# A list-scheduled transformer block: routed experts in freed places, one factor to ScalarE, and a new set of due times

## The chip, the cores and the metric
The kernel runs on one core of one Trainium2 chip, in one launch. The metric is the device time of that core in microseconds. Its engines are called by the short names that the profile uses: PE is TensorE (PEld its weight loads), DVE is VectorE, ACT is ScalarE, POOL is GpSimd, SP is SyncE, whose queue issues all the kernel's DMAs.

## The reference
64 sequences of 256 tokens with 256 features, each with a context of 120 tokens, pass through four steps, each added to the tokens under a tanh gate:

```python
x = x + tanh(g_xattn[0]) * L0_xattn(layernorm(x), ctx)   # 16 heads of 64, softmax over 120
x = x + tanh(g_ffn[0])   * L0_ffn(layernorm(x))          # 8 experts, gate softmax, threshold 0.1
x = x + tanh(g_xattn[1]) * L1_xattn(layernorm(x), ctx)   # 16 heads of 16
x = x + tanh(g_ffn[1])   * L1_ffn(layernorm(x))          # 8 routed experts, two of them per token
```

The last step has 512 routing rows only, so it applies to the first 512 tokens (one group). For them each routed expert computes, with LIMIT = 7 and alpha = 1.702:

```python
gate = minimum(x @ Wg + bg, LIMIT)
up   = clip(x @ Wu + bu, -LIMIT, LIMIT)
y    = ((up + 1) * gate * sigmoid(alpha * gate)) @ Wd + bd      # weighted and summed by token
```

All arithmetic is in float32.

## The kernel before
**Work and order.** Tokens are taken in 32 groups of two sequences (512 tokens, four tiles of 128). One group is one *turn*, and its work falls into three stages: *front* (keys and values of the context, first attention), *middle* (`ffn0`, the gated experts) and *back* (second attention, then the store). The group with the routed experts, group 0, is taken as the third from last. Its own fourth step, `ffn1`, comes at the very end as the stage *routed*.

**The planner.** The code does not issue instructions directly. Each piece (four matmuls, one copy, one DMA) is a `step` with an engine, a cost in us, the steps it comes after, the buffers it opens and uses, and a due time. The class `Plan` runs a list schedule over all steps: whenever an engine falls idle in the model, the ready step with the earliest due time is taken, if its buffers are free. The instructions are then emitted in that order, and each engine executes its own in that order. The due time of a step comes from its place in its stage: `begin + length * (PE time before it / PE time of the stage)`, in turns, less a correction from the table `EARLY` (thousandths of a turn, one number per step; positive is earlier). The constants `FRONT`, `MIDDLE`, `BACK` and `ROUTED` hold begin and length.

**Tile shapes on PE.** Most matmuls use the full 128x128 array; scores, values and gate logits use smaller tiles, and each has a `mode` (`scores0`, `values0`, `scores1`, `values1`, `logits`). The planner adds a cost when the mode changes, and shifts due times: `ALONE` when the only ready tiled step would enter from full work, `PAIR` when there are several, `BACK` for going back to full, `OTHER` from one tiled mode to another.

**Softmax weights** are transposed by DMA (`by_dma`): POOL splits the words into halves (tile `hv`), SP issues the transpose into `tu`, ACT joins the halves into `aT` or `aTb` (line 733). Layer norms of the middle and back, and of later fronts, go the same way. In the model a transpose occupies SP for 2.6 us and is seen 2.0 us after that.

**Buffers** are rings of places. Those that matter here: `x_ring` (4 token places), `xn_ring` (2, normalized tokens, 1024 words a row), `exf_ring` (4, first attention's weights `ex`), `q0_ring` (3, queries `qT`), `v0_ring` (2), `ao0_ring` and `k0_ring` (1 each), `late_ring` (2, of which second attention uses three in turn), `sp_ring` (2 score places in PSUM) and `mm_ring` (4 PSUM banks).

**Routed experts** (`ffn1`). An expert's gate and up matrix is loaded into a place of `v0_ring`, the down matrices into the one place each of `ao0_ring` and `k0_ring`. For each half `m` of the hidden features: a PE step for gate and one for up; DVE takes each out of PSUM with bias and upper limit into a place of `exf_ring` (line 1502); ACT makes a tanh of the gate (line 1511); POOL clips the up factor from below and adds one (line 1518); DVE makes gate times (tanh + 1) (line 1525); POOL multiplies the two factors into a place of `q0_ring` (line 1534). Two PE steps then multiply by the down matrix, and DVE adds to the tokens with the routing weight (line 1564). The loads, and the normalization of the routed tokens, come after `front_done`: the last group's whole front.

Of the kernel before, what the change touches and what calls it, by code (L numbers as in the profile page):

```python
# [13 lines left out]
AF = mybir.ActivationFunctionType  # L14
# [3 lines left out]
P = 128  # L18
D = 256
NQ = 256  # L20
# [16 lines left out]
FRONT, MIDDLE, BACK = (0.0, 1.183), (1.177, 0.93), (1.839, 1.446)  # L37
ROUTED = 6.144
# [3 lines left out]
        -598, -378, -110, -125, -80, 105, 286, 614, 655, -721, 157, 99, -416, -870, -204, 264,  # L42
        -122, 142, -893, -81, -1097, -217, -1070, 136, -768, 416, 276, 99, 625, 512, 251, 565,
        324, 395, -10, 52, -142, -190, -26, 408, 780, 198, -182, 86, -27, -432, 40, 893, 828,
        -519, -46, 248, -49, -395, -279, -29, 632, 812, 1061, 763, -242, 337, 265, -203, 742, 961,
        932, -681, 722, 367, 194, 309, 264, -40, -361, -149, -83, -766, -372, -340, -367, -208,
        -289, -483, -398, -30, 787, 935, -284, -594, 415, -438, -47, 851, 536, -306, -60, 312,
        -214, 279, -581, -1304, -287, -457, -295, -126, -1285, -557, -508, 107, -303, 230, -727,
        -735, -366, -421, -491, 481, 112, -803, 25, 34, -278, -347, 458, 177, -689, -626, -456,
        -883, -321, -547, -840, -697, -1162, -735, -571, -1139, -1160, -491, -1203, -322, -536,  # L50
        -595, -737, -459, -140, -820, -745, -152, 266, 200, -291,
    ],
    "front": [
        243, 272, -206, -364, -216, 241, 53, 106, -149, 513, -137, 189, -424, 1037, -307, -271,
        -85, 67, -427, 13, -118, -471, 50, -39, 390, 203, -231, -469, -807, -273, 207, -264, 703,
        217, 296, 299, 13, 600, 256, -650, -10, -437, -167, 243, 332, 341, 216, 159, -72, 335, 96,
        370, 351, 196, 75, 1040, 364, -197, -303, 280, -478, 232, 35, 77, 105, -225, -473, -384,
        -152, 890, 304, 612, -1015, 634, 408, 258, 342, -115, 671, 252, 76, -125, 66, 60, -307,
        -279, -374, -614, -294, -449, -310, -72, -378, -440, -641, -499, -356, 274, 536, 197,
        -287, 744, 158, 473, 163, -827, 931, 730, -3, -215, -1626, 51, -98, 2, 31, 175, -1228,  # L60
        -672, -648, -422, -406, 392, 731, -68, -169, -1092, -201, -623, -32, -494, 633, -924,
        1305, 84, -517, 373, -1350, 217, -384, -656, 516, -497, 680, 350, 324, 1955, 421, 1294,
        531, 1216, 698, -1274,
    ],
    "middle": [
        -121, -494, 280, 1233, 936, 1977, 1723, 2493, 1181, 484, 955, 763, 1384, 1719, 1131, 1958,
        870, 1018, 1132, 2801, 1132, 1078, 1100, 2346, 1538, 1394, 1665, 1992, 1197, 1040, 964,
        982, 1137, 1192, 1414, 1123, 931, 511, 488, 503, 497, -121, -252, -98, -272, 5, -372,
        -223, -706, -428, -304, -633, -870, -314, -620, -1258, -431, -892, -219, -256, -519, -865,
        -264, -264, -814, -255, -704, -658, -174, -600, -476, -279, -350, -317, -97, 33, -159,  # L70
        -247, -773, -86, -224, -761, 358,
    ],
    "back": [
        776, 1052, 901, 505, 1125, 1001, 1083, 1445, 691, 154, 600, -72, -298, -196, -382, -714,
        -669, -132, 174, -270, -92, -405, 578, 595, 405, 235, 1862, 498, 1543, 217, -311, 62,
        -512, -609, -676, -361, -324, 850, -318, -655, -147, 203, 244, -8, 370, -48, -247, 349,
        -213, -369, -506, 1037, 35, -139, -1632, -791, -1054, -121, -311, 585, -495, -874, 111,
        324, 870, 589, 1263, 263, 142, 863, 667, 170, -501, 902, 17, 406, 1429, 101, -48, -1162,
        -1300, -801, -94, -268, -195, -1010, -726, -590, 210, 990, -81, 290, -303, 506, 68, 155,
        898, 644, 699, 20, -45, -908, -320, -1047, 136, 717, 822, 818, 1051, 1457, 1006, 1157,  # L80
        392, 1644, 605, 1267, 1187, 676, 1428, 749, 611, 384, 193, 2225, -188,
    ],
    "routed": [
        711, 592, 528, 855, -6, -59, -332, -372, 8, -431, -662, -133, 3, -622, -262, -45, -735,
        201, -188, -813, -90, -232, 452, -778, -354, -329, -159, -737, -207, 489, 159, -203, -375,
        -172, 254, -1016, -1038, 703, 698, 1382, 631, 643, 244, 39, 694, 355, -425, 405, -1062,
        656, 3, 123, -237, -528, -600, -368, -817, 554, -108, -226, -58, -181, -634, -1383, -1354,
        -455, -1053, -1286, 800, 184, 1457, 155, 1203, 357, 473, 191, -503, 23, 1480, -93, 2097,
        491, 435, 875, -62, 102, -294, -939, 36, -1066, -1043, 841, -363, 1840, -500, 1298, -771,
        -436, -149, -425, -401, 2073, -917, 2078, 20, -189, -259, -325, -648, -1304, -2133, -761,  # L90
        -1974, -1761, 336, -1255, 1315, -1191, 1517, 51, 714, 863, -214, 39, 1984, -305, 1422,
        -641, -209, 1216, 459, 439, -453, -440, 474, -1091, -893, 1257, -862, 1798, -953, 1308,
        -570, -380, 137, -43, -885, 1373, -840, 1205, -1003, -423, -139, -542, -1195, -2086,
        -2446, -1272, -2493, -2435, 164, -1449, -45, -1537, 330, -301, -906, -62, -1961, -1313,
        -484, -2129, 18, -1342, -1790, -860, -1268, -1911, -2954, -2491, -1495, -2770, -2495, 47,
        -1622, 595, -2026, 212, -186, -243, 352, -546, -1385, 530, -901, 428, 101, -121, 464, 464,
        -164, -892, -1105, -550, -1699, -1435, 883, -848, 1063, -1202, -128, 470, -950, -187,
        -870, -1407, -121, -1037, -40, -803, -982, -63, -1031, -747, -982, -659, 228, -1432, -930,
        1609,
# [7 lines left out]
BY_DMA_SEEN = 2.0  # L107
TURN = "FBM"
HALVES, TURNED, XNS = 2, 2, 2
BEHIND1 = 0  # L110
# [35 lines left out]
class Plan:  # L146
# [10 lines left out]
        "logits": 0.154, "bias": 0.16,  # L157
    }


    ALONE, PAIR, BACK, OTHER = 0.283, -0.055, 0.357, -0.066
# [6 lines left out]
    def step(self, engine, us, emit, after=(), opens=(), uses=(), mode="full", port=False,  # L168
        kind=None, seen=None):
        s = Step(engine, us, emit, after, opens, uses, mode, port)  # L170
        s.due, s.kind, s.seen = self.at, kind, seen or self.SEEN[engine]
        if engine == "PE":
            self.at += us
        self.stage.append(s)
        return s
# [11 lines left out]
    def ordered(self):  # L187
# [7 lines left out]
        port_from = 0.0  # L195
        done = []
# [8 lines left out]
        while events:  # L205
# [15 lines left out]
            while started:  # L221
                started = False
                for e, steps in waiting.items():
# [42 lines left out]
                    heapq.heappush(events, (now + us + s.seen, next(number), s))  # L266
# [18 lines left out]
def kernel(  # L285
# [42 lines left out]
    def ring(name, n, *shape):  # L328
# [19 lines left out]
        ring(name, *((2, P, 8 * P) if which in BY_DMA else (4, P, 2 * NQ)))  # L348
        for name, which in (("aT", "0"), ("aTb", "1"))
# [366 lines left out]
    def by_dma(ex, n, aT, after, which, of_halves=()):  # L716
# [15 lines left out]
        def joined():  # L732
# [9 lines left out]
            "SP", 2.6, lambda: nc.sync.dma_start_transpose(tu.tile, hv.tile),  # L742
            [s], opens=[tu] if of_halves else [tu, aT], uses=[hv, *of_halves], kind="D" + which,
            seen=BY_DMA_SEEN,
# [35 lines left out]
    def add_bias(tk, gated_bias, after):  # L780
        tk.change(
            range(NT), "POOL", 2.385,
            lambda: nc.gpsimd.tensor_tensor(
                tk.x.tile, tk.x.tile,
                gated_bias.unsqueeze(1).to_broadcast([P, NT, D]), ALU.add,
            ),
            after,
        )

    def context0(tk):  # L790
# [31 lines left out]
        for b in range(NB):  # L822
# [29 lines left out]
            vs.append((v, v_in))  # L852
        return kT, kT_in, vs

    def attention0(tk, xnT, xnT_in, kT, kT_in, vs, behind=1):
        nch = NC0 // 2

        def queries(b, hf):
            qTs = []
            for c2 in range(nch // 2):  # L860
# [17 lines left out]
                )  # L878
                s = step(
# [38 lines left out]
        def attend(b, hf, exs, ao):  # L918
            v, v_in = vs[b]
            made = []  # L920
            for u, (ex, s) in enumerate(exs):
# [38 lines left out]
                )  # L960
                c = hf * nch + u * 2
# [71 lines left out]
    def bias_folded():  # L1033
# [39 lines left out]
        s = step("PE", 0.42, gate_mean, gw_in, opens=[ps], mode="logits")  # L1073
# [9 lines left out]
    def ffn0(tk):  # L1083
# [4 lines left out]
        def logits_T():  # L1088
# [13 lines left out]
            mode="logits",  # L1102
# [295 lines left out]
    def ffn1(tk, after):  # L1398
# [42 lines left out]
        ]  # L1441
        xnT = Held(xnT_rings[0])
        xnT_in = layernorm_T(tk, xnT, after, which="routed")
# [3 lines left out]
        for e in range(NE):  # L1447

            def dn_of(e):
# [8 lines left out]
                    after, opens=[] if e % 4 else [dns[e // 4]],  # L1458
# [3 lines left out]
        for e in range(NE):  # L1462
            gu = Held(v0_ring)

            def gu_of(gu=gu):
# [7 lines left out]
                after, opens=[gu],  # L1473
            )
            hTs = [Held(q0_ring) for _ in range(2)]
            hT_in = []
            for m in range(2):
                made = []
                gate, up, sig = Held(exf_ring), Held(exf_ring), Held(aTf_ring)
                for s in range(2):  # L1480
                    ps = Held(mm_ring)

                    def project(m=m, s=s, ps=ps, gu_of=gu_of):
# [11 lines left out]
                    into = up if s else gate  # L1495
                    p = step(
                        "PE", 1.716, project, [*xnT_in, gu_in],
                        opens=[ps, into] if s else [ps, into, sig, hTs[m]], uses=[gu, xnT],
                    )

                    def bounded(e=e, m=m, s=s, ps=ps, into=into):
                        return nc.vector.tensor_scalar(
                            into.tile[:, :TOK], ps.tile, gub_s[:, e, s, m : m + 1], LIMIT,
                            ALU.add, ALU.min,
                        )
# [172 lines left out]
```

## Time and profile before
| what | us |
|---|---|
| median of three runs (lowest, highest) | 3569.85 (3568.73, 3570.05) |
| the profiled execution | 3568.64 |
| its span, first to last instruction | 3566.9 |
| PE busy | 3501.9 |
| DVE, ACT, POOL busy | 2828.2, 2481.6, 2398.9 |
| routed gate and up out of PSUM by DVE (line 1502), 32 instructions | 23.8 |
| PE waits for the routed product on POOL (line 1534), 6 times | 15.0 |

The page's span is the time between the first and the last instruction; the profiled execution's own time has 1.7 us more around it. A line number stands for the place in the code, and since a helper issues nearly all matmuls, they all have line 545: groups are told apart by tiles, as in `mm<-ew,xnT_m` (the gated experts), `mm<-xnT_f,v` (routed gate and up), `mm<-kT,qT` and `mm<-ao,qT` (routed down), `sp<-kbd,late` and `mm<-aTb,vsp` (scores and values of the second attention), `mm<-xnT_m,gw` (gate logits). PE counts as busy over the modelled ends of its matmuls.

### The profile page before, as it was taken

How to read it: one execution, taken by the hardware profiler on the slowest of the kernel's cores; microseconds unless marked ns; L12 is line 12 of the kernel's file. 1: busy time of each engine (PE TensorE's matmuls, PEld its weight loads, DVE VectorE, ACT ScalarE, POOL GpSimd, SP SyncE). 2: the span in 40 equal slices, each digit the busy share in tenths (PEclk: the TensorE clock that was granted, in tenths of full speed). 3: DMA queues.
4: the chain of work that ended last, by engine and by line, in shares of the span. 5: the costliest groups of instructions: out<-in, count | busy, mean ns of one | idle time of the engine just before them, and what ended most of it. 6: DMA issues, size and time to landing. Idle time of an engine off the chain costs nothing.

```text
span 3566.9 us, 52784 instructions
## 1 busy us (share of the span) xinstructions
PE 3501.9 (98%) x20053; PEld 2261.0 (63%) x20053; DVE 2828.2 (79%) x4981; ACT 2481.6 (70%) x2230; POOL 2398.9 (67%) x1625
## 2 busy tenths in 40 slices
PE   7999999999999999999999999999999999999987
PEld 5756666666666666666666666666666666666544
DVE  6677778888777888777888777888877888877776
ACT  4666677777677777677777677777767777767643
POOL 5556667676667776667666667767666777666666
PEclk9999999999999999999999999999999999999998
DMA  6445565555555565555655555555555556555633
GB/s 173 79 83 103 104 113 103 104 110 110 105 109 104 107 115 104 104 108 106 110 109 108 105 102 114 103 106 110 109 100 114 104 107 113 106 102 99 125 71 83
DMA packets 1300861, 378.26 MB, mean 106 GB/s; under 512 B 1266144, under 2 KB 1280896, under 8 KB 1300608
## 3 DMA queue, kind: packets, MB, share of 16 engines
q1 hardware_dynamic: 1300608, 374.90, 54.9%
q8 instruction: 157, 2.57, 0.3%
q14 instruction: 96, 0.79, 0.1%
HBM read 39.80 MB, written 16.78 MB: 16 GB/s over the span
## 4 chain that ended last, share of the span: by engine, by line
PE 84%; DVE 6%; DMA 3%; issue 3%; POOL 3%; ACT 2%; POOLq 0%; SPq 0%; DVEq 0%; ACTq 0%
PE mm L545 74%; PE sp L545 10%; DMA tu<-hv 3%; DVE sum L684 2%; DVE sum L669 1%; POOL hv L724 1%; DVE exb L674 1%; ACT aTb L733 1%; POOL exb L693 1%; ACT aT L733 1%; DVE xt L1187 0%; ACT exb L679 0%; DVE xt L776 0%; DVE ln L571 0%; POOL ex L1518 0%
## 5 line engine op out<-in xcount | busy, mean ns | idle before, releaser
L545 PE MATMUL mm<-ew,xnT_m 128*128 128x512 f32 x2048 | 952.7, 596 | 6.1 <-DVE xt L776 4.1
L733 ACT COPY aTb<-tu 120x2048 uint16<-120x2048 uint16 x256 | 637.5, 2502 | 186.0 <-DMA tu<-hv 184.8
L693 POOL TENSOR_TENSOR exb<-exb,sum 128x960 f32<-128x960 f32 x256 | 460.4, 1803 | 425.4 <-DVE sum L688 420.2
L1187 DVE SCALAR_TENSOR_TENSOR xt<-mm,w_s,xt 128x256 f32<-128x256 f32 x1024 | 486.7, 478 | 265.1 <-PE mm L545 247.1
L733 ACT COPY aT<-tu 120x2048 uint16<-120x2048 uint16 x256 | 636.7, 2505 | 78.7 <-DMA tu<-hv 78.6
L669 DVE TENSOR_REDUCE sum<-sp 128x8 f32<-128x960 f32 x512 | 575.8, 1141 | 113.3 <-PE sp L545 111.1
L693 POOL TENSOR_TENSOR ex<-ex,sum 128x960 f32<-128x960 f32 x256 | 458.2, 1796 | 263.2 <-DVE w_s L1141 132.7
L545 PEld LDWEIGHTS mm<-ew,xnT_m 128*128 128x128 f32 x2048 | 382.2, 190 | 358.1 <-issue 311.5
L545 PE MATMUL mm<-xnT_f,wq 128*128 128x256 f32 x2048 | 489.8, 387 | 0.4 <-DVE xt L1187 0.4
L545 PE MATMUL mm<-wo,ao 128*128 128x256 f32 x2048 | 466.7, 384 | 0.0
L724 POOL COPY hv<-ex 128x1920 uint16<-128x1920 uint16 x256 | 455.2, 1786 | 17.0 <-DMA tu<-hv 12.9
L724 POOL COPY hv<-exb 128x1920 uint16<-128x1920 uint16 x256 | 455.2, 1785 | 6.6 <-DMA tu<-hv 0.3
L545 PEld LDWEIGHTS mm<-xnT_f,wq 128*128 128x128 f32 x2048 | 376.1, 190 | 98.9 <-issue 44.8
L545 PEld LDWEIGHTS mm<-wo,ao 128*128 128x128 f32 x2048 | 381.7, 190 | 79.6 <-issue 31.1
L684 DVE TENSOR_REDUCE sum<-exb 128x8 f32<-128x960 f32 x256 | 287.9, 1136 | 67.8 <-ACT exb L679 67.5
L684 DVE TENSOR_REDUCE sum<-ex 128x8 f32<-128x960 f32 x256 | 289.3, 1141 | 16.4 <-ACT ex L679 16.4
L545 PE MATMUL mm<-wv,ct 128*120 128x512 f32 (+1 forms) x768 | 300.5, 528 | 0.0
L545 PEld LDWEIGHTS sp<-kT,qT 64*128 64x128 f32 x4096 | 242.3, 188 | 87.8 <-issue 74.9
L674 DVE TENSOR_TENSOR ex<-sp,sum 128x960 f32<-128x960 f32 x256 | 289.6, 1143 | 0.6
L545 PE MATMUL mm<-ct,wk 128*128 128x240 f32 x1280 | 289.8, 371 | 0.0
L545 PEld LDWEIGHTS mm<-ct,wk 128*128 128x128 f32 x1280 | 242.0, 191 | 70.5 <-issue 53.3
L674 DVE TENSOR_TENSOR exb<-sp,sum 128x960 f32<-128x960 f32 x256 | 286.1, 1147 | 0.0
(117 smaller groups left out, 4603.3 us busy)
## 6 DMA issues: line engine op xcount, KB each, us to landing
xt<-in_x SPq DMA_DIRECT2D x32, 512.0 KB, 4.3
out_x<-xt SPq DMA_DIRECT2D x32, 512.0 KB, 2.8
tu<-hv SPq DMA_TRANSPOSE x607, 4.4
ct<-in_ctxT SPq DMA_DIRECT2D x32, 240.0 KB, 2.7
v<-in_gu_w SPq DMA_DIRECT2D x8, 512.0 KB, 4.3
ew<-in_expert_w SPq DMA_DIRECT2D x2, 1024.0 KB, 9.6
wk<-in_wkT SPq DMA_DIRECT2D x1, 1024.0 KB
wv<-in_wvT SPq DMA_DIRECT2D x1, 1024.0 KB
```

The costliest lines, as they stand in the source:

```text
L545: return [nc.tensor.matmul(**t) for t in terms]
L669: lambda: nc.vector.tensor_reduce(per_head(0), scores(), AX.X, ALU.max),
L674: lambda: nc.vector.tensor_tensor(weights(), scores(), wide(0), ALU.subtract),
L684: lambda: nc.vector.tensor_reduce(per_head(8), weights(), AX.X, ALU.add),
L693: lambda: nc.gpsimd.tensor_tensor(weights(), weights(), wide(8), ALU.mult),
L724: return copy[APART[which][0]](hv.tile.rearrange("p (h c n) -> p h c n", h=2, c=8)[:, :, :, :n], ex.tile.bitcast(U16).rearrange("p (c n h) ...
L733: return copy[JOINED[which][0]](flat().bitcast(U16).rearrange("p (c n h) -> p h c n", h=2, c=8)[:n], tu.tile[:n].rearrange("p (h c) n -> p ...
L1187: return nc.vector.scalar_tensor_tensor(xs, ps.tile[:, i * D : (i + 1) * D], w.tile[:, t, e : e + 1], xs, ALU.mult, ALU.add,)
```

## The change
- **Routed experts' places.** The products of odd experts go to a token place (`x_ring`), those of even experts stay in `q0_ring`. The factors of the second half (`m = 1`) share one place of `xn_ring`, those of the first stay in two places of `exf_ring`. Places are opened later: the tanh's at the tanh, the product's at the product.
- **When they may begin.** The routed normalization comes after the last group's last query step, the gate and up loads after its last value step, the down loads after its last first-output step, in place of `front_done`.
- **Upper factor.** ACT takes it out of PSUM with its bias, to which DVE adds one once; POOL then clips to (1 - LIMIT, 1 + LIMIT). DVE keeps the gate.
- **Gate tiles.** The mode `logits` is gone; the gate steps have mode `values1`.
- **The model.** Transposes take 1.9 us of SP and are seen 2.4 us later, and none lands within 3.5 us of the one before. The four shifts for tiled steps change.
- **Due times.** New begins, lengths and corrections for all stages; the last group's middle and back have tables of their own.

The numbers of steps and of matmuls per group stay as they are. The core of the diff, without the tables:

```diff
-FRONT, MIDDLE, BACK = (0.0, 1.183), (1.177, 0.93), (1.839, 1.446)
-ROUTED = 6.144
+FRONT, MIDDLE, BACK = (0.0, 1.174), (1.208, 0.757), (1.866, 0.888)
+ROUTED = 6.482
...
-BY_DMA_SEEN = 2.0
+BY_DMA_SEEN = 2.4
...
-        "logits": 0.154, "bias": 0.16,
+        "bias": 0.16,
     }
-    ALONE, PAIR, BACK, OTHER = 0.283, -0.055, 0.357, -0.066
+    SPACED = 3.5
+    ALONE, PAIR, BACK, OTHER = 0.656, 0.033, 0.572, 0.052
...
+                    end = now + us + s.seen
+                    if s.spaced:
+                        end = landed = max(end, landed + self.SPACED)
...
-            "SP", 2.6, lambda: nc.sync.dma_start_transpose(tu.tile, hv.tile),
+            "SP", 1.9, lambda: nc.sync.dma_start_transpose(tu.tile, hv.tile),
...
-            mode="logits",
+            mode="values1",
...
+        up_in = [step("DVE", 0.2, lambda: nc.vector.tensor_scalar(
+            gub_s[:, :, 1, :], gub_s[:, :, 1, :], 1.0, None, ALU.add), gub_in)]
-        xnT_in = layernorm_T(tk, xnT, after, which="routed")
+        xnT_in = layernorm_T(tk, xnT, [front["queries"]], which="routed")
...
-                    after, opens=[] if e % 4 else [dns[e // 4]],
+                    [front["output"]], opens=[] if e % 4 else [dns[e // 4]],
...
-                after, opens=[gu],
-            )
-            hTs = [Held(q0_ring) for _ in range(2)]
+                [front["values"]], opens=[gu],
+            )
+            if e % 2:
+                hTs = [Held(x_ring)] * 2
+            else:
+                hTs = [Held(q0_ring) for _ in range(2)]
...
-                gate, up, sig = Held(exf_ring), Held(exf_ring), Held(aTf_ring)
+                sig = Held(aTf_ring)
+                held = [Held(xn_ring)] * 2 if m else [Held(exf_ring) for _ in range(2)]
...
+                    def biased(ps=ps, factor=factor, b=b):
+                        return nc.scalar.activation(factor(1), ps.tile, AF.Identity, bias=b)
...
+                    if s:
+                        made.append(step("ACT", 0.69, biased, [p, *up_in], uses=uses))
+                    else:
+                        made.append(step("DVE", 0.747, bounded, [p, *gub_in], uses=uses))
...
-                        up.tile[:, :TOK], up.tile[:, :TOK], -LIMIT, 1.0, ALU.max, ALU.add
+                        factor(1), factor(1), 1.0 - LIMIT, 1.0 + LIMIT, ALU.max, ALU.min
...
-        plan.end_stage(turn + MIDDLE[0], MIDDLE[1], EARLY["middle"])
+        plan.end_stage(turn + MIDDLE[0], MIDDLE[1], EARLY[last + "middle"])
...
-        plan.end_stage(turn + BACK[0], BACK[1], EARLY["back"])
+        plan.end_stage(turn + BACK[0], BACK[1], EARLY[last + "back"])
```

`front["values"]`, `front["queries"]` and `front["output"]` are set in `context0` and `attention0` and hold the last such step that was made, that is, the last group's.

## Prediction
> **What bounds the kernel now.** I read the page first, then stretches of 20 us, then TensorE in order of time in one middle turn and in the last 200 us, and last the waits.
>
> ```profile
> span 3566.9 us, 52784 instructions
> PE 3501.9 (98%) x20053; PEld 2261.0 (63%) x20053; DVE 2828.2 (79%) x4981; ACT 2481.6 (70%) x2230; POOL 2398.9 (67%) x1625
> PE   7999999999999999999999999999999999999987
> PEclk9999999999999999999999999999999999999998
> ```
> TensorE is the bound; only the first slice and the last two are not full. There are two places to gain: what TensorE spends inside the full stretches, and the ends.
>
> TensorE inside one middle turn (start us, us, what):
> ```profile
> 1042.85 1.07 PE L545 MATMUL mm<-aTb,vsp 120*32 120x256 f32 x16
> 1043.85 1.99 PE L545 MATMUL mm<-xnT_f,wq 128*128 128x256 f32 x8
> 1045.68 1.89 PE L545 MATMUL mm<-wv,ct 128*120 128x256 f32 x8
> 1047.50 0.64 PE L545 MATMUL mm<-xnT_m,gw 128*32 128x128 f32 x16
> 1048.07 1.98 PE L545 MATMUL mm<-ew,xnT_m 128*128 128x512 f32 x4
> ...
> 1061.61 1.88 PE L545 MATMUL mm<-ew,xnT_m 128*128 128x512 f32 x4
> 1063.42 1.09 PE L545 MATMUL sp<-kbd,late 32*128 32x240 f32 x16
> 1064.44 3.72 PE L545 MATMUL mm<-xnT_f,wq 128*128 128x256 f32 x16
> ```
> Starts tell more than durations. Twelve undisturbed expert products elsewhere (1075.48 to 1080.72, 5.24) give 1.72 for four, against 1.81 before the tiled work at 1063.42: entering costs about 0.09. The eight products from 1043.85 take 1.82; eight clean ones of their size 1.72 (32 output products, 3346.81 to 3353.91, take 7.10 with both sides): leaving costs about 0.1. A second value step behind a first adds 0.86 where one alone adds 1.02: a change of tile shape costs about 0.155. A turn of this plan has 12 entries and 19 groups of one shape, so 12 x 0.2 + 19 x 0.155 = 5.3 us of its 105.6 (gate products start at 1047.50 and, a turn later, at 1153.1). Of 30 such distances 17 are 105.6; others reach 107.0.
>
> The end (20 us rows: busy PE, PEld, DVE, ACT, POOL, clock, DMA), then its TensorE rows, then its waits:
> ```profile
> 3340.00:3360.00 20.00, 20.00 (x103) 12.13 (x102) 15.37 (x32) 12.97 (x9) 12.08 (x9) 1.00 0.62 114
> 3360.00:3380.00 20.00, 12.35 (x60) 6.85 (x59) 9.82 (x28) 10.93 (x8) 10.72 (x11) 0.74 0.87 212
> 3520.00:3540.00 20.00, 13.94 (x70) 7.70 (x68) 17.60 (x23) 9.28 (x8) 17.00 (x10) 0.95 0.34 63
> 3540.00:3560.00 20.00, 15.53 (x68) 10.66 (x68) 8.23 (x14) 10.17 (x8) 10.29 (x6) 0.71 0.28 52
> ```
> ```profile
> 3367.64 1.93 PE L545 MATMUL mm<-aTb,vsp 120*32 120x256 f32 x16 [5.64 <-ACT aTb L733]
> 3540.02 6.01 PE L545 MATMUL mm<-kT,qT 128*128 128x256 f32 x16 [4.79 <-POOL qT L1534]
> 3553.82 5.50 PE L545 MATMUL mm<-kT,qT 128*128 128x256 f32 x14 [4.45 <-POOL qT L1534]
> 3559.26 1.07 PE L545 MATMUL mm<-aTb,vsp 120*32 120x256 f32 x16
> ```
> ```profile
> PE mm L545 <- POOL qT L1534: 15.0, 6, 4.8
> PE mm L545 <- ACT aTb L733: 11.2, 4, 5.6
> PE mm L545 <- DMA v<-in_gu_w: 2.6, 1, 2.6
> ```
> From 3355 on TensorE idles 32.4 us (8.4 in the 3245 us before that, 19.7 in the first 110). It also runs slow: the down products read from kT take 503 ns each here, against 384 for the same shape in the middle (the wo,ao group). The steps after 3355 at clean durations (19 expert and 32 gate or up steps of 1.72, 16 down steps of 1.73, 17 of scores or values at 0.86, queries 6.9, outputs 8.6, others 7) make 152 us in 207; the other 55 are 32 idle, about 7 of shape changes, 16 lost to low clock and waiting weights. The work that idles is the eight routed experts, each waiting for its own product on GpSimd, and the second attention of turns 30 and 31.
>
> **The change, part by part.** Sums go against the profiled execution, 3568.64 us (span 3566.9 and 1.7 around it); the median of the three runs is 1.2 above it.
>
> *Routed start.* The normalization now needs the last queries (3316), the expert loads the last values and first output products, instead of the whole front (3355). The loads are as many, 8 of 512 KB and 8 of 256 KB, about 0.5 us of SP's queue each. Before, ten of them crowd 3351 to 3374: DMA share 0.87, and the transpose for the value step at 3367.64 is late behind them. SP works in order, so a load that waits for its place holds transposes queued behind it, and with them ScalarE's join and the value step: at worst 5.4 us, the longest wait of aTb. The v places come free only with turn 31's own value steps (by 3346), kT at 3321, ao at 3354, so about half the crowd moves. What fills the 5.64 us hole is a gate or up product that could not start until 3389. Between -7 (hole and wait for weights) and +5; taken -5, nearest the hole itself.
>
> *Places.* Odd experts' products go to a token place, the second half's factors to a normalization place: two experts in flight instead of one and a half. This attacks the 15.0 us on qT. Between 0 (turn 30's token place is free only after its store, near 3480, and one place serves until then) and -15. Four of the six waits, 11.9 us, come after 3499, when two places are free: taken -9. An odd product waits for the store that reads its place, 2.8 us to land on the page; GpSimd's copies and their transposes stand behind it. Hidden while the store is turns old, otherwise up to +3.
>
> *Clock.* Slow down products cost 64 x (503 - 384) + 64 x (411 - 384) ns = 9.3 us. Gone if all pauses go, kept if none do: taken -4, as for half.
> The Trainium skill, "TensorE: Matmul & The Clock Gate", Part 1, says that an idle window of 3.4 us halves the clock until a busy window has passed. By it only the pauses of 5.64, 4.79 and 4.45 cost, an estimated 1.7 us each, 5.1 together, and half of that would be -2.5 in place of -4. The row at 3360 (clock 0.74 after the hole) agrees in kind.
>
> *Upper factor.* 16 VectorE steps of 747 ns (12.0 us) leave; 16 ScalarE steps of 512 columns with a bias, as L1281's 687 ns, come: 11.0 us. GpSimd keeps one tensor_scalar. ScalarE is under 11 of 20 busy in these rows, VectorE up to 17.6, and VectorE feeds the scores: 0 to -6, taken -2. If ScalarE's cover went, a join would be late by 0.69. The one addition to the bias is 0.2 us on VectorE.
>
> *Own due times of the last group.* They let turn 31's scores go ahead of down products; the last value step stands behind one that waits 4.45. 0 to -10, taken -3. Sum for the end: -23; its floor, all idle and slow time gone, is -48.
>
> *Plan.* Steps and matmuls of a turn stay; the order changes. The model takes 1.9 us of SP for a transpose, its rows near 3360 show 1.8 to 1.9 (2.6 before), and 4.3 from issue to landing; the page says 4.4. The price of a lone tiled step rises from 0.283 to 0.656 turns, and gate products count as values. In the turn shown 6 of 12 entries bring one step. Gate products beside a value step would save 0.35 (entry, exit and shape); another merge 0.2. Bounds per turn: -0.75 and, if every turn had the waits of the worst, 107.0 - 105.8 = +1.2; over 30 turns -22 to +36. I take one merge in most turns, -8, the nearest row being the gate's own 0.57 against a clean 0.42.
> The Trainium skill, "TensorEngine Tiling (Array Packing)", Key Properties, says that a change of tiling mode drains TensorE and a change of tile alone does not. The rows call the gate 128*32 and the values 120*32, so by it the pair is free: -0.35 a turn, -10.5. No run here has shown them side by side.
>
> Total 3568.64 - 23 - 8 = 3537.6, and at the median 3538.8: 3539.
>
> **Rivals.** *Scores held back (slower).* Second attention is a chain: queries at 1055.2, four score steps 23, 17 and 18 us apart, last output at 1158.2, the next queries at 1160.8. It fills the turn. A score step takes both score places, so it is often alone and pays the raised price. Shortest distances of about 16 us leave some 10 us a turn of slack (7 + 1 + 2); once hold-ups exceed that, each us is a us in all 30 turns. One us over: 3569.85 + 30 - 23 = 3577. For it: no slack at the turn's end. Against it: only 8.4 us of idle in 3245.
> *The end hardly moves.* Eight score rounds of 17 us bind the last 180 us, and fillers only fill: -5 and -2, no merges, 3563 or a little above. *All of it:* half the distance to the end's floor more (-40) and -22: 3508. *The edit is dead:* if the planner starts no routed work before 3385, result 3566 to 3573.
>
> **Numbers.** Forecast case 0.48, all of it 0.14, held scores 0.22, hardly moves or dead 0.16 (9 of these faster by more than 0.2%, which is 7 us and about what repeated runs can tell; 7 within). Faster 0.71, same 0.07, slower 0.22. The range, 3506 to 3580, leaves out half of the slow case and the best of the good one; the likeliest case's own range is 3518 to 3555.
>
> **What would show it.** Right: idle time of TensorE after the last front under 18 us; the qT wait under 7; routed products within 10 us of 3350; 11 or fewer entries a turn, the gate beside values; turns of 105 us or less; 16 VectorE steps fewer in the routed line and 16 of 0.69 us on ScalarE. Wrong: turns over 106 with idle at value steps (held scores), the last eight score rounds still 17 us apart (the end), or transposes waiting on SP behind loads.

## The result and the profile after

The change makes the kernel slower. Its median is 3584.77 us (six runs, 3582.51 to 3586.64) beside 3569.51 for the kernel before on the same chip (six runs, 3568.54 to 3572.53): ratio 1.0042, 95% interval 1.0029 to 1.0054. The forecast was 3539, with a range up to 3580. The profiled execution took 3585.22 us, 1.7 more than its span.

The page of the changed kernel, the lines that answer to those shown of before:

```profile
span 3583.5 us, 52821 instructions
PE 3508.6 (98%) x20053; PEld 2253.4 (63%) x20053; DVE 2800.8 (78%) x4966; ACT 2497.2 (70%) x2246; POOL 2399.8 (67%) x1625
PE   7999999999999999999999999999999999999898
PEclk9999999999999999999999999999999999999999
```

The instructions moved as the diff says: 15 fewer on VectorE (16 factors go, one addition comes), 16 more on ScalarE. The clock dip of the last slice is gone. But the span is 16.6 us longer while TensorE is busy only 6.7 us more, and the page cannot say where, since a loss of 0.7% shows in no digit of it.

What shows it is a ruler. Every turn has one gate product, so the starts of the gate products of turns 0 to 31 cut both spans alike (us):

| stretch | before | after | difference |
|---|---|---|---|
| start to the gate of turn 0 | 152.1 | 158.3 | +6.2 |
| gate of turn 0 to that of turn 2 | 153.8 | 151.8 | -2.1 |
| turn 2 to turn 29 (27 turns) | 2861.0 | 2882.3 | +21.3 |
| turn 29 to turn 30 | 105.6 | 105.7 | +0.1 |
| gate of turn 30 to the end | 294.4 | 285.4 | -9.0 |

So the end did improve, and two places where the prediction had put a gain or nothing lost more. (The expectations below call the gate of turn 2 "the second", counting from zero, and have 294.3 and -8.9 for the end, from a rounded span. Their mean turns, and those given with experiments 10 to 12, are over the 26 turns from the gate of turn 2 to that of turn 28.) The middle's 21.3 has two parts. The shortest distance between gates is 105.58 us before and 105.73 after: 27 x 0.15 = 4.1. That agrees with one more change of tile shape in each turn (32 instead of 31, counted in the traces), at the 0.155 us that the prediction read for one. Above the shortest, the 27 turns add up to 10.3 us before and 27.5 after: 17.2. Fourteen turns of before are within 0.2 us of the shortest, and three of after.

**The start.** One TensorE row of the changed kernel, in order of time (start us, us; in brackets the idle time before it):

```profile
87.74 0.45 PE L1039 MATMUL mm<-ident,w 128*128 128x128 f32 x1 [3.57 <-DVE w L1470]
```

This is the transpose of the routing weights, a piece of `ffn1`. Before ran it near 3360 us. The new plan runs it in the first turn, where it waits for VectorE, which makes the weights from routing indices whose load it had itself waited for (0.71 us), and all of TensorE's queue waits behind it. After the wait TensorE's clock is low as well: 0.50 between 87 and 90 us.

**The middle.** Which TensorE instructions wait, and what ScalarE waits for, between 310 and 3190 us (us in total, times, longest), first before, then after:

```profile
PE mm L545 <- DVE xt L776: 3.8, 8, 0.7
PE mm L545 <- ACT aT L733: 2.6, 6, 0.6
...
ACT v L846 <- PE mm L545: 152.2, 55, 3.6
ACT aTb L733 <- DMA tu<-hv: 143.5, 163, 2.9
ACT qT L881 <- PE mm L545: 140.5, 125, 2.9
ACT ao L965 <- PE mm L545: 101.2, 119, 2.9
ACT late L1281 <- PE mm L545: 62.2, 56, 1.2
ACT kT L815 <- PE mm L545: 58.5, 37, 2.7
ACT aT L733 <- DMA tu<-hv: 45.2, 33, 2.9
ACT late L1373 <- PE mm L545: 35.2, 28, 1.3
```
```profile
PE mm L572 <- ACT xnT_f L760: 3.2, 9, 1.2
PE mm L572 <- ACT kT L844: 2.6, 4, 0.9
PE mm L572 <- ACT late L1406: 2.4, 3, 1.0
PE sp L572 <- ACT qT L912: 2.3, 5, 0.8
PE mm L572 <- DVE xt L1220: 2.2, 3, 0.9
PE sp L572 <- DVE exb L701: 1.6, 5, 0.4
...
ACT aTb L760 <- DMA tu<-hv: 207.0, 109, 7.2
ACT late L1314 <- PE mm L572: 152.8, 27, 5.8
ACT exb L706 <- DVE exb L701: 108.4, 98, 2.8
ACT aT L760 <- DMA tu<-hv: 87.1, 61, 2.9
ACT qT L912 <- PE mm L572: 71.5, 85, 2.0
ACT ao L998 <- PE mm L572: 69.1, 101, 1.2
...
ACT late L1406 <- PE mm L572: 25.2, 55, 0.5
ACT kT L844 <- PE mm L572: 16.8, 24, 0.8
...
ACT v L875 <- PE mm L572: 3.6, 16, 0.2
```

No TensorE wait is large; there are more kinds of them. TensorE's idle time in this stretch grew from 7.1 to 16.0 us; the rest of the 10.3 and 27.5 us stands in what the profile counts as busy, and is not split further here.

The ScalarE rows suggest why. Its idle time as a whole is the same (788 us before, 794 after); what it stands before has changed. It waits for transposes of weights (`aT`, `aTb`) 294 us instead of 189, and for VectorE's scores (`ex`, `exb`) 136 instead of 27. In return it waits for TensorE, over all its copies out of PSUM, 339 us instead of 550; for the first queries, the keys and the gathered outputs alone (`qT`, `kT`, `late` of L1406, before L1373) it is 113.5 us in 164 waits instead of 234.2 in 190. Time in which ScalarE waits for TensorE can serve as a reserve: after a late transpose it can catch up there. Of this reserve the new order has 211 us less, and about half of that now stands before transposes, the other half before VectorE. What it has more of is one long wait a turn, for the second attention's queries (L1314, 27 times up to 5.8 us; before, 56 short ones at L1281), which can help only at that place. The reading to be tested is this: the copies behind a late join come late to TensorE, and so `kT`, `late` and `qT`, which are plain copies out of PSUM, appear as things that TensorE waits for.

One such place, ScalarE and TensorE of the changed kernel in order of time:

```profile
2511.65 2.52 ACT L760 COPY xnT_f<-tu 128x2048 uint16<-128x2048 uint16 x1 [0.59 <-DMA tu<-hv]
2514.02 0.57 ACT L844 COPY kT<-mm 128x480 f32<-128x480 f32 x1
2514.23 3.72 PE L572 MATMUL mm<-xnT_f,wq 128*128 128x256 f32 x16
2514.46 2.53 ACT L760 COPY aT<-tu 120x2048 uint16<-120x2048 uint16 x1
```

The join waits 0.59 us for its transpose and ends at 2514.17; the queries start at 2514.23. By these rows 0.06 us were to spare, and a landing later than that would hold up the queries and the `kT` copy behind the join. In one turn of before the same join ended 1.25 us ahead of its queries (2617.62 and 2618.87).

**The gate.** TensorE around a gate product, after:

```profile
2442.73 1.89 PE L572 MATMUL mm<-wv,ct 128*120 128x256 f32 x8
2444.55 0.65 PE L572 MATMUL mm<-xnT_m,gw 128*32 128x128 f32 x16
2445.13 1.13 PE L572 MATMUL mm<-ew,xnT_m 128*128 128x512 f32 x2
```

Full work on both sides, as before; so it is in 31 of the 32 turns. In no turn of the changed kernel's trace does a gate product stand beside the second attention's values.

**The end.** A row of 20 us (busy PE, PEld, DVE, ACT, POOL, clock, DMA), then TensorE in order of time, then its two largest waits from 3340 us on:

```profile
3540.00:3560.00 20.00, 15.02 (x68) 8.34 (x67) 13.70 (x18) 11.29 (x12) 17.55 (x11) 0.91 0.28 53
```
```profile
3402.03 1.99 PE L572 MATMUL mm<-wo,late 128*128 128x256 f32 x8 [1.74 <-ACT late L1406]
...
3417.97 3.60 PE L572 MATMUL mm<-xnT_f,v 128*128 128x512 f32 x8
...
3570.24 5.67 PE L572 MATMUL mm<-kT,xt 128*128 128x256 f32 x14 [4.11 <-POOL xt L1601]
3575.84 1.07 PE L572 MATMUL mm<-aTb,vsp 120*32 120x256 f32 x16
```
```profile
PE mm L572 <- POOL xt L1601: 4.1, 1, 4.1
PE mm L572 <- POOL qT L1601: 4.1, 1, 4.1
```

The clock in this row is 0.91 where it was 0.71. The wait for routed products on GpSimd fell from 15.0 us in six to 8.2 in two. The routed work itself starts no earlier: its first product is at 3417.97, and it follows the second attention of its own group, whose last output starts at 3402.03 (before: 3373.06, first product 3388.71).

### The profile page after: what moved, and what is told of

Its sections match the earlier page's. It is cut to its first block, busy times and chain, and to the rows that moved or that the text cites. A ratio compares the mean times of both kernels' runs of the same rounds, so it can differ in the third digit from the quotient of the medians.

```text
span 3583.5 us, 52821 instructions
## 1 busy us (share of the span) xinstructions
PE 3508.6 (98%) x20053; PEld 2253.4 (63%) x20053; DVE 2800.8 (78%) x4966; ACT 2497.2 (70%) x2246; POOL 2399.8 (67%) x1625
## 4 chain that ended last, share of the span: by engine, by line
PE 62%; DVE 16%; DMA 7%; POOL 6%; ACT 4%; issue 4%; SPq 1%; POOLq 0%; DVEq 0%; ACTq 0%
PE mm L572 55%; PE sp L572 7%; DMA tu<-hv 6%; DVE sum L711 4%; DVE sum L696 3%; POOL ex L720 2%; POOL hv L751 2%; DVE xt L1220 2%; DVE ex L701 2%; DVE xn L639 2%; DMA xt<-in_x 2%; DVE exb L701 1%; ACT xnT_f L760 1%; SPq L769 1%; POOL exb L720 1%
## 5 line engine op out<-in xcount | busy, mean ns | idle before, releaser
L572 PE MATMUL mm<-wo,ao 128*128 128x256 f32 x2048 | 456.8, 381 | 0.7 <-ACT ao L998 0.7
L706 ACT ACTIVATE exb<-exb 128x960 f32<-128x960 f32 x256 | 256.2, 1005 | 128.8 <-DVE exb L701 128.5
L706 ACT ACTIVATE ex<-ex 128x960 f32<-128x960 f32 x256 | 256.9, 1006 | 50.8 <-DVE ex L701 47.1
```

The costliest lines, as they stand in the source:

```text
L572: return [nc.tensor.matmul(**t) for t in terms]
L706: lambda: nc.scalar.activation(ex.tile, ex.tile, AF.Exp, scale=scale),
```

## The experiments

Kernels named "pinned" keep the planned order of every engine, and an added function moves chosen steps by so many us. Where only part of an order is changed, the rest stays.

**1. Routing weights later.** The changed kernel with the routing weights' step and its transpose on TensorE 100 us later.

```diff
+    if stage == 130 and i in (33, 34):     # the routing weights' transpose and its copy
+        return 100.0
```

> The changed kernel with one edit in its order: the transpose of the routing weights on TensorE and its copy on ScalarE stand about 100 us later. In the changed kernel TensorE sits 3.6 us in front of that transpose at 84 us, behind a late load. Theory (arrivals that the plan counts as earlier than they are, with TensorE's order fixed): the start shortens by the idle time and the slow clock after it, first gate products back from 158.3 to about 153, total -4 to -6: 3579 to 3581. Rival (the start is not on the path, later waits take it up): 3584 to 3586.

Measured: 3579.71 us median, ratio 1.0036 (1.0024 to 1.0049). The first gate product starts at 152.5 instead of 158.3 us (before: 152.1). Of the +6.2 of the start 5.7 are this one step; the middle stays at 2881.1.

**2. GpSimd's split of the front's tokens one step earlier**, so that their transpose, for which the queries wait (`xnT_f`, the largest of TensorE's rows above), goes out earlier.

```diff
+    if part == 0 and 1 < turn < 31 and i == 30:     # hv<-xn of the front
+        return -3.0
```

> The changed kernel with one edit in its order: in every turn GpSimd splits the front's normalized tokens one step earlier, ahead of a multiplication of 1.8 us that has slack; their transpose, ScalarE's join and the first queries on TensorE keep their places. Theory (the first queries have no slack behind this transpose, and each late landing is paid by TensorE): about 0.45 us a turn back, turns of 106.2 in place of 106.7, total -8 to -13: 3572 to 3577. Rival (the turn's length is the sum of shapes and entries, waits only move to the next arrival): within 3 of 3584.8.

Measured: 3580.64 us, ratio 1.0034 (1.0021 to 1.0047). The queries' wait (3.2 us) is gone, but the 27 turns take 2877.4, only 4.9 us less and not the 12 that were expected. TensorE's waits for `kT` (3.3 us), `late` (2.6), `qT` (2.2) and VectorE's token sums (2.2) stand much as they were. This single wait was not the cause of most of the loss.

**3. VectorE's first statistics later.** In the changed kernel VectorE waits for a token load 21 times (14.2 us), and other work of its queue stands behind.

```diff
+    if part == 0 and 1 < turn < 30 and 16 <= i <= 23:     # statistics of loaded tokens
+        return 5.0
```

> The changed kernel with one edit in its order: in every turn VectorE reads the newly loaded tokens for their first statistics 5 us later, so that the load has landed. In the changed kernel VectorE waits 14.2 us for these loads in 21 turns. Theory (late arrivals): the wait goes, and about a third of it was passed to TensorE: -3 to -6, 3579 to 3582. Rival (VectorE, busy 78%, takes the wait up by itself): 3583 to 3586.

Measured: 3592.07 us, ratio 1.0067 (1.0053 to 1.0081). The wait for the load fell to 0.5 us, and the kernel became slower: the shortest turn grew from 105.73 to 106.01. Both expectations missed it. TensorE's wait for VectorE's token sums grew from 2.2 to 4.1 us, so what stands behind the statistics in VectorE's queue seems to have had no room to come later; no run tests that further.

**4. All three together.**

> The three edits together. Theory (late arrivals): they add up, -15 to -25, 3560 to 3570, and the time of the kernel before is reached or passed, since the end is shorter than before's. Rival (waits move on): 3578 to 3583.

Measured: 3581.39 us, ratio 1.0038 (1.0025 to 1.0050). That is the rival's range: the gains do not add, and the 27 turns take 2882.2. Taking away waits one by one leads nowhere here, so the next runs ask what the waits have in common.

**5. Order of before, end of after.** The changed kernel's code, with the order of before written out up to the gate product of turn 30 and the changed order behind it.

```diff
-    for s in plan.ordered():
+    for s in walked(plan.ordered(), moved):     # moved: WANTED[step] - s.start
```

> All of the order of before up to the gate product of turn 30, written out by hand, and from there the changed kernel's order; the code is the changed kernel's. The changed kernel's trace against before's shows the span split in three: +6.2 us at the first gate product, +21.3 from the second to the one of turn 29, -8.9 from the gate product of turn 30 to the end (294.3 to 285.4 us). Slack theory: the loss is the turns' order, and the end's gain is the end's own; it stays if before's turns stand in front: 3558 to 3562 us where before has 3567 to 3570, the span from the gate of turn 30 at 284 to 288 us. Rival: the end is only short because the turns in front of it handed it work that was further on; then the stretch stays at 291 us or more and the time at 3566 to 3575.

Measured: 3561.81 us (3560.51 to 3566.48, eleven runs) beside 3569.37: ratio 0.9980 (0.9971 to 0.9989). It beats both kernels. The 27 turns take 2862.2, as in before; from the gate of turn 30 to the end it is 289.4 us, between the two expectations, in a profiled execution of 3566.48 that was the longest of the eleven. So the loss of the middle is the order of the turns, and of the end's gain the profile shows about half (4.9 of 9.0 us) with before's turns in front.

**6 and 7. Transposes of half the blocks, in before and in after.** The transposed tiles' other halves are left out.

```diff
-            "SP", 1.9, lambda: nc.sync.dma_start_transpose(tu.tile, hv.tile),
+            "SP", 1.9, lambda: nc.sync.dma_start_transpose(tu.tile[:, :8], hv.tile[:, : 8 * P]),
```

> Before, its order pinned, with each DMA transpose moving the first half of its blocks only (the other half of the transposed tokens and heads is left out and the tiles hold zeros there), so that transposes land earlier. A mean turn of before is 105.98 us, an undisturbed one 105.58. Slack theory: turns fall to 105.6 to 105.7. Rival (order and shapes of the products, engine load): 105.9 or more. This run is the base for the changed kernel with the same halves.

> The changed kernel, its order pinned, with the same halves left out of each DMA transpose. Its mean turn is 106.74 us, an undisturbed one 105.73. Slack theory: late landings of transposes are what its order cannot absorb, so turns fall to 105.75 to 105.9, and the stretch from the second gate product to the one of turn 29 stands 0 to 6 us above that of before with the same halves (21.3 us with whole transposes). Rival: the waits come of the copies out of PSUM and VectorE's own order; the stretch stays 13 us or more above.

Measured: the median from issue to landing falls from 4.4 and 4.3 us to 3.0 and 3.1. Before takes 3557.96 us and every one of its 27 turns is the shortest, 105.58. After takes 3554.63 and 25 of its 27 turns are within 0.2 us of 105.73. The 27 turns take 2850.7 and 2856.2: of the middle's 21.3 us 5.5 are left, of which 4.1 is the longer shortest turn. With these transposes the change would be a gain, 3.3 us by one run of each. That is the slack theory's case and excludes the rival's 13. Executions with one order of the turns agree within 2 us over these 27 turns (2861.0, 2862.2 and 2860.8 with before's, in before and experiments 5 and 9; 2882.3, 2881.1 and 2882.9 with the changed one, in after and experiments 1 and 8), so one profile of each carries such differences.

**8. The upper factor back on VectorE**, in the changed kernel, pinned.

```diff
-                        return nc.scalar.activation(factor(1), ps.tile, AF.Identity, bias=b)
+                        return nc.vector.tensor_scalar(factor(1), ps.tile, b, None, ALU.add)
```

> The changed kernel, its order pinned, with the routed experts' upper factor taken out of PSUM by VectorE again (16 instructions) where the change has ScalarE do it. Theory: in the end the chain of score rounds binds and neither engine does; the time differs from the changed kernel's by -1 to +3 us. Rival (VectorE feeds that chain, and the move to ScalarE is worth most of the end's 8.9 us): +5 to +10 us.

Measured: 3589.91 us, ratio 1.0056 (1.0041 to 1.0072). The end from the gate of turn 30 grows from 285.4 to 289.7 us, so ScalarE's part of it is about 4.3, nearer the rival than the theory. The two ratios' intervals overlap; the profile carries this one.

**9. The upper factor alone.** Before, pinned, with nothing of the change but the factor on ScalarE.

```diff
+                        if s:
+                            return nc.scalar.activation(
+                                into.tile[:, :TOK], ps.tile, AF.Identity,
+                                bias=gub_s[:, e, s, m : m + 1])
...
-  up.tile[:, :TOK], up.tile[:, :TOK], -LIMIT, 1.0, ALU.max, ALU.add
+  up.tile[:, :TOK], up.tile[:, :TOK], 1.0 - LIMIT, 1.0 + LIMIT, ALU.max, ALU.min
```

> One part of the change alone: before, its order pinned, with the routed experts' upper factor taken out of PSUM by ScalarE (16 instructions), 1 added to its bias once and GpSimd clamping on both sides, as the change has it. With the upper factor back on VectorE the changed kernel's end from the gate product of turn 30 grew from 285.4 to 289.7 us. Theory: the factor lies on the chain from product to GpSimd, and VectorE's queue in front of it is what is saved; in before too, and the end falls by 3 to 6 us from 294.3, the time to 3563 to 3567 beside 3569. Rival: in before the chain waits for places (the wait for GpSimd's qT, 15.0 us in 6), which a quicker factor does not open; the end stays within 1.5 us and the time at 3567 to 3571.

Measured: 3571.71 us beside 3568.75, ratio 1.0008 (0.9999 to 1.0017); the end takes 296.1 us (294.4 before). Its largest TensorE wait from 3250 us on:

```profile
PE mm L613 <- POOL qT L1612: 15.8, 4, 5.6
```

The theory is excluded. The result lies a little above the rival's bounds (1.7 us for 1.5 in the end, 3571.71 for 3571), and the wait for `qT` stays (15.0 us before): that fits the rival, by which before's chain waits for places that a quicker factor does not open. So the factor, costed at -2, was worth nothing on its own and 4.3 us of the end together with the rest of the change; that the freed places are what it needs is likely, but no run frees them alone.

**10 and 11. Half blocks for the tokens' transposes only, and for the weights' only** (the other halves of these are left out), in the changed kernel (`which` is "L" for tokens, "0" and "1" for the two attentions' weights).

```diff
+                if which in "L"      # in the other kernel: "01"
+                else nc.sync.dma_start_transpose(tu.tile, hv.tile)
```

> The changed kernel, order pinned, with only the transposes of normalized tokens moving half their blocks (the other half is left out). Whole transposes give a mean turn of 106.77 us, halves of all kinds 105.79. If the tokens' transposes carry the loss (their wait, the queries' for the turned tokens, is the largest single one, 6.5 of the 16 us): 106.0 to 106.2. If it is spread over all arrivals, in proportion to the transposes quickened: 106.4 or more.

> The changed kernel, order pinned, with only the transposes of the two attentions' weights moving half their blocks. If the tokens' transposes carry the loss: a mean turn of 106.5 or more. If the loss is spread over all arrivals and lies in how busy SP's queue and the DMA engines are, the weights' being most of the 19 transposes of a turn: 105.8 to 106.1.

Measured, one run of each: 3579.15 and 3557.50 us beside 3568.75 for before, with mean turns of 106.57 and 105.85 us. Above 27 shortest turns stand 22.4 and 3.2 us (27.5 with whole transposes). So 5.1 and 24.3 us are gone, close to the shares of these transposes in a turn (3 and 16 of 19, or 4.3 and 23.2 us): the loss is spread over the transposes, and the weights' carry most of it, although TensorE hardly ever waits for a weights tile itself. (The 6.5 us that the first expectation gives for the queries' wait is not in the rows above, which have 3.2.) Waits of the kernel with the weights' halves, 310 to 3190 us:

```profile
PE mm L640 <- ACT xnT_m L828: 0.4, 1, 0.4
PE mm L640 <- ACT xnT_f L828: 0.2, 1, 0.2
...
ACT aTb L828 <- DMA tu<-hv: 118.5, 31, 4.7
ACT qT L984 <- PE mm L640: 104.7, 108, 2.0
...
ACT kT L916 <- PE mm L640: 54.2, 54, 1.0
ACT late L1478 <- PE mm L640: 39.5, 77, 0.6
...
ACT aT L828 <- DMA tu<-hv: 18.4, 30, 2.1
```

ScalarE stands 137 us before transposes instead of 294, has 198 us of reserve at `qT`, `kT` and `late` instead of 113.5 (475 instead of 339 over all copies out of PSUM), and TensorE's waits for all three are gone. Two readings were left: ScalarE's queue hands the delay on, or the landings themselves hold other engines.

**12. Shorter joins, whole transposes.** The join of a weights tile on ScalarE copies the upper 16 bits of each number only (the lower are left out).

```diff
-                flat().bitcast(U16).rearrange("p (c n h) -> p h c n", h=2, c=8)[:n],
-                tu.tile[:n].rearrange("p (h c) n -> p h c n", h=2),
+                flat().bitcast(U16).rearrange("p (c n h) -> p h c n", h=2, c=8)[:n, FROM[which] :],
+                tu.tile[:n].rearrange("p (h c) n -> p h c n", h=2)[:, FROM[which] :],
```

> The changed kernel, order pinned, whole transposes, but the copy that joins the halves of a turned weights tile on ScalarE (2.50 us, 16 of the 19 joins of a turn) writes the upper halves of the numbers only (the lower 16 bits are left out and stay zero). The transposes land as late as before; ScalarE has some 1.2 us less to do for each. Theory (a late landing costs PE because ScalarE, in order, stands in front of its other copies and has no spare time to catch up; halving the weights' transposes gave back its waits for PE): mean turns of 105.8 to 106.1 beside 106.77. Rival (the landings themselves, by values steps and by VectorE's rows, hold PE): 106.4 or more.

Measured, in one run: 3572.74 us beside 3571.16 for before, and a mean turn of 106.09 us; 9.3 us stand above 27 shortest turns, so 18.2 of 27.5 are gone. (Its start is 5.4 us longer than the changed kernel's, from clearing four tiles once.) A join takes 1.35 us instead of 2.50. Its waits, 310 to 3190 us:

```profile
PE sp L643 <- DVE exb L772: 1.7, 5, 0.4
PE mm L643 <- ACT xnT_f L831: 1.2, 3, 0.5
...
ACT aTb L831 <- DMA tu<-hv: 201.2, 100, 7.2
...
ACT qT L983 <- PE mm L643: 160.7, 135, 2.0
...
ACT aT L831 <- DMA tu<-hv: 121.9, 63, 3.8
ACT late L1477 <- PE mm L643: 98.5, 94, 1.6
ACT kT L915 <- PE mm L643: 52.9, 54, 1.0
```

Here the transposes are as late as ever (323 us of ScalarE's waiting, and a median landing of 4.4 us), yet TensorE's waits for `kT`, `late` and `qT` are gone, and ScalarE has 312 us of reserve at these copies (682 over all). That settles about two thirds: late landings cost TensorE time because ScalarE takes its queue in order and the new order leaves it too little reserve to catch up. The remaining third went with quick landings (experiments 7 and 11) and did not go with shorter joins; its largest rows here are `exb` and `xnT_f`, and by which way it reaches TensorE is not shown.

## Why the prediction was wrong

**The plan (-8, measured +21.3 in 27 turns, +19.2 with the two before them).** This is the step that failed. I costed an order that I had not seen by its shape changes alone, and took one merge a turn as gained. None came: a turn has 12 entries as before and 32 changes of shape instead of 31, and the gate was never beside the values, so the gain that was read out of the relabelled mode had no object. Waits in the middle entered only through the bound of +1.2 a turn. I took "only 8.4 us of idle in 3245" as an argument against a slower result. It was a property of that one order, which met its landings with ScalarE's reserve, and the new order did not keep it: what stands above the shortest turn went from 10.3 to 27.5 us, which is 17.2 of the 21.3. Shorter joins on ScalarE took 18.2 of the 27.5 away (experiment 12), quick landings all but 1.4 (experiment 7). What the Trainium skill, "TensorEngine Tiling (Array Packing)", Key Properties, says of a change of tile within one tiling mode is shown for this pair by no run here, since no gate stood beside a value step of the second attention.

**The start (nothing, measured +6.2).** The prediction listed the loads of `ffn1` and forgot its early pieces. The diff moves every step's due time, so each step without a predecessor in the last group could be moved to any place. Experiment 1 puts 5.7 of the 6.2 down to one transpose.

**Routed start (-5, for a reason that did not hold).** The wrong wait was taken for the binding one. Freed of `front_done`, the routed work still follows its own group's second attention, and with the last turn 117.4 instead of 102.8 us long that ends later, not earlier: the first routed product starts 119.9 us after the gate of turn 30, where it was 116.1, and not near 3350. The hole that the term went by did close: TensorE's waits for `aTb` from 3250 us on fell from 11.2 to 0.2 us. The ten loads that stood between 3351 and 3374 now stand between 3359 and 3401, which may be the reason; no run takes this part alone, so what it was worth is open.

**Places (-9) and clock (-4).** About right by the rows: the waits for routed products fell by 6.8 us, and the down products cost 32 x (477 + 444 + 382 + 379) ns = 53.8 us instead of 64 x (503 + 411) ns = 58.5, so 4.7 less. The reading that only the three longest pauses slow the clock does not fit before's own rows: the clock is 0.53 from 3462.6 to 3466.2 us after a pause of 2.62, and 0.65 from 3503.0 to 3507.8 after one of 2.41, but 1.00 from 3488.3 to 3491.8 after one of 2.45.

**Upper factor (-2).** Right in sign, 4.3 in size, and nothing without the rest of the change (experiments 8 and 9). **Own due times (-3)** can't be told apart from the rest of the end.

**The end as a whole (-23, measured -9.0).** The parts were added as if each stood on the path. The rival "the end hardly moves" (-5 and -2) was nearer: after, the last eight score rounds are still two chains of four, 13 to 20 us apart in each (3497.59, 3514.28, 3532.84, 3545.74 the last four), and the last value step, with the output behind it, still ends the chain.

**Two readings of the rows were off** without bearing on this. The twelve expert products said to be undisturbed stand before tiled work, so their 5.24 us hold an entry; less the four with an entry (1.81), the other eight give 1.72 for four, as stated. And 15 of the 31 distances between gate products are 105.6 us, not 17 of 30.

**The slow rival** said 3577 and named the right place, an over-full turn, with a price of 1 us a turn where 0.8 was measured. That its total came within 8 us of the result is in part luck, since it had the end at -23. Its mechanism was another: score steps held back for lone entries. Steps held back by the order should lengthen every turn, but with quick landings 25 of 27 turns of the same order are at its shortest, 105.73 us, only 0.15 above before's (experiment 7).

Still open is which edit of the planner took ScalarE's reserve: the transposes' new prices, the shifts for tiled steps, the gate's mode or the new due times. Each alone gives another order everywhere, with tables that were made for none of them, and it was not tried.

## What to carry to other kernels

When an order written by a planner is replaced, do not cost it by its shape changes or its sum of work: ask for each in-order queue how long it now stands before transfers and how much waiting it has left to catch up, because that waiting on an engine at 70% can be a reserve and not waste. Many small waits for different plain copies of one engine can have one cause that stands ahead of them in that engine's queue, as most of them had here; removing one of them gained little, and three edits at once no more. A ruler through the span (one product per turn) finds a 0.7% loss that no share of busy time shows, and here it also showed that the two halves of the change could be had apart: before's turns with the new end run at 3561.8 us, 0.2% faster than before.

## What the runs showed of the hardware

A transpose by DMA between on-chip tiles took 4.3 to 4.4 us from issue to landing, and with half the blocks still 3.0 to 3.1, so by an estimate, if the rest goes with its size, some 1.7 us of it does not; SP's time for issuing one fell from 1.91 to 1.23 us. Halving the transposes took the DMA share of the middle slices from five or six tenths to two or three, and with it every TensorE wait of before's 27 turns went to zero: in the kernel before, all 10.3 us lost in these turns went with the transposes, at a load where the page shows the DMA engines half idle.
